# Routing tokens of two mixture-of-experts layers by scatter into expert regions of DRAM, with resident expert weights

## The chip, the cores and the metric

The kernel runs on one core of a Trainium2 chip. The metric is the device time of one execution in microseconds. The core has a matrix engine (PE, with its weight loads shown as PEld), a vector engine (DVE, `V` in the code), a scalar engine (ACT, `S`), a general engine (POOL, `G`), and an engine that only issues transfers (SP); each works through its own queue in order. Below, "us" are microseconds from the start of the profiled span.

## The reference

The input is x, 16 batches of 128 tokens with 128 features, and a condition and a context of 77 tokens per batch. All is float32. Four blocks are added to x one after the other:

```python
x = x + xcond0(layernorm(x), cond, ctx)    # self-attention, cross-attention, gated FFN (GLU)
x = x + ffn0(layernorm(x))                 # 1 shared + 7 routed experts, 2 of the 7 per token
x = x + xcond1(cond, ctx, layernorm(x))    # slot attention over the context, 3 turns
x = x + ffn1(layernorm(x))                 # 8 experts, 1 per token
```

An expert of ffn0 is `silu(h @ g.T) * (h @ u.T) @ d.T` with 352 inner features, weighted per token by the two scores normalised to one. An expert of ffn1 is `relu(h @ W1 + b1) @ W2 + b2` with 512 inner features, weighted by the largest softmax probability. Only the chosen experts have to be computed for a token.

## The kernel before, in words

The residual x is held on chip as `r`, 128 partitions by 16 batches by 128 features, and is worked on in four groups of four batches. After both attentions (to about 433 us) come, for each group, the GLU (`glu`, L1283) and the routing of ffn0 (`moe0_route`, L930); the routing of group g-1 is written after the GLU of group g. Then come the sort of all tokens by expert (`sort`, L757), the shared expert on the four groups (`moe0_shared`, L958), the tiles of the routed experts (`tiles`, L879), the slot attention (`slot_turns`), the routing of ffn1 (`moe1_route`, L1194), its sort and its tiles. Outside of what a program line demands, the framework that builds the program orders instructions on each engine; it also puts in the waits.

Routing a group (`normed`, L733) normalises it into a staged tile `st`, transposes it, multiplies by the router's weights and forms one-hot rows of the chosen experts (`oh`); `any` is their sum and `cum` a running count. `rows` (L746) writes the staged rows to a DRAM table (`tok0`, `tok1`) in token order, by SP; each row ends with the token's weight, and in ffn1 also holds the residual.

`sort` needs all four groups. Two matmul calls give every token its rank among those of its expert. Each expert's list is padded to full tiles of 128, which makes at most 38 tiles in ffn0 (2 x 2048 tokens over 7 experts) and 23 in ffn1 (2048 over 8). From rank and expert start comes the place of each token. The inverse list, which token stands at each place, is formed by one-hot rows over the lanes (`la`, L827) and products (`tv`, L817 and L822) as bf16 matmuls. Its results are `to`, the row that a tile's output goes to, `frm`, the row its input comes from, and `row`, the row of its expert's weights. In ffn1 two strings of matmuls into a scratch tile (`busy`, L798), whose results are not used, stand between its steps.

A tile j then has this path. `fetch` (L867): POOL gathers its 128 rows by an indirect transfer (L874); in ffn0 12 are issued ahead of the loop, in ffn1 6. `weights` (L855): SP loads the expert's row number into a register (L861) and issues a 576 KB load of that expert's weights (L864) into one of six buffers. `turn` (L885): PE transposes the tile, ACT copies it out. `up`: in ffn0 (L972) 6 matmuls, a tanh on ACT and two DVE operations (`silu_gate`, L950); in ffn1 (L1224) 4 matmuls, two ReLU halves on ACT and two on DVE. `finish` (L890): the down product (3 or 4 matmuls), its scaling, the next `weights`, a POOL scatter of the results (L895) and the next `fetch`. In ffn0 the scaling is on ACT with `wk`, a column that DVE makes for each tile (L987); in ffn1 it is two DVE operations (L1248, L1249). The loop writes up of tile j, turn of tile j+1, then finish of tile j-1. In ffn0 results go to a table `res0` of two rows per token; `combine` (L915) reads both (`yg`) and adds them to `r` by matmuls with the identity, at the start of the slot attention. In ffn1 they go to the output.

In the tables, `gum` and `h1n` are the up products, `ynm` and `ynn` the down products, with m for ffn0 and n for ffn1; `zsm`, `zsn` are fetched tiles, `ysm`, `ysn` results.

Of the kernel before, what the change touches and what calls it, by code (L numbers as in the profile page):

```python
# [31 lines left out]
WBUFS = 6  # L32
WT = 1156
NTOK = B * P
FETCH = 7
# [22 lines left out]
def pixart_kernel(  # L58
# [61 lines left out]
    for b in range(2, B, 2):  # L120
# [13 lines left out]
    tok0 = dram.tile([NTOK, D + 1], F32, name="tok0")  # L134
    tok1 = dram.tile([NTOK, 2 * D + 1], F32, name="tok1")

    res0 = dram.tile([2 * NTOK + NT0 * P, D], F32, name="res0")

    y_row = const.tile([P, 2 * B + NT0], F32, name="y_row")
    G.iota(  # L140
        y_row, pattern=[[P, y_row.shape[1]]], base=0, channel_multiplier=1, allow_small_or_imprecise_dtypes=True
    )
    zero_sb = attc.tile([P, D], F32, name="zero_sb")
    G.memset(zero_sb, 0.0)
    dma(out=res0[0:P, :], in_=zero_sb)

# [489 lines left out]
    def wide(nm):  # L636
# [3 lines left out]
    wt = ctx.enter_context(tc.tile_pool(name="wt", bufs=WBUFS))  # L640
    rt = ctx.enter_context(tc.tile_pool(name="rt", bufs=1))
    slp = ctx.enter_context(tc.tile_pool(name="slp", bufs=1))
    ctxn = slp.tile([NC, B, D], F32, name="ctxn")
    dma(out=ctxn, in_=ctx_tok.rearrange("b n d -> n b d"))
    cb = slp.tile([P, B, D], F32, name="cb")
    dma(
        out=cb,
        in_=rows[0, R_COND * D : (R_COND + B) * D].partition_broadcast(P).rearrange("p (b d) -> p b d", d=D),
    )


    def glu_body(g, hT):
        u = ph.tile([P, 4, 512], F32, name=f"u{g}", tag="act")
        for c in range(4):
            ps = {}
            for j in (1, 0):
                ps[j] = wide(f"glu{g}_{c}_{j}")
                PE.matmul(ps[j], lhsT=gluw[:, 4 * j + c, :], rhs=hT, start=True, stop=True)
            ge = ph.tile([P, 512], F32, name=f"ge{g}_{c}", tag="gate")
            S.activation(ge, ps[1], AF.Gelu, bias=col(C_FFB1 + 4 + c))  # L660
            V.scalar_tensor_tensor(u[:, c, :], ps[0], col(C_FFB1 + c), ge, ALU.add, ALU.mult)
        y = psX.tile([P, 4, D], F32, name=f"yg{g}", tag="x")
        token_major(y, lambda c: u[:, c, :], lambda c: gluw[:, 8 + c, :], 4)
# [36 lines left out]

    jt = rt.tile([P, NTM], F32, name="jt")
    G.iota(jt, pattern=[[1, NTM]], base=0, channel_multiplier=0, allow_small_or_imprecise_dtypes=True)

    w_issue = []

    batch_row = rt.tile([P, 2 * B], F32, name="batch_row")
    G.iota(batch_row, pattern=[[-1, 2 * B]], base=2 * B, channel_multiplier=0, allow_small_or_imprecise_dtypes=True)
    lanes = rt.tile([P, P], BF16, name="lanes")
    G.iota(lanes, pattern=[[1, P]], base=0, channel_multiplier=0, allow_small_or_imprecise_dtypes=True)

    class Routed:


        def __init__(self, nm, ne, nk, w, w0, tok):
            self.nm, self.ne, self.nk, self.w, self.w0, self.tok = nm, ne, nk, w, w0, tok
            self.ws, self.zs, self.st = [], {}, {}
            self.b0, self.nb = 0, B
            nb = self.nb
            self.nt = n_tiles(nk * nb * P, ne)
            self.oh = self.tile([P, nk, nb, ne], "oh")  # L720
            self.any = self.tile([P, nb + 1, ne], "any")
            self.cum = self.tile([P, nb + 1, ne], "cum")
            V.memset(self.any[:, nb, :], 0.0)
            V.memset(self.cum[:, 0, :], 0.0)
# [7 lines left out]

        def normed(self, i, nm):  # L733

            g = self.b0 // 4 + i
            rg = r[:, 4 * g : 4 * g + 4, :]
            rs, mean = ln_stats(rg, P, 4, nm, g)
            self.st[i] = rt.tile([P, 4, D + 1], F32, name=f"st{nm}", tag="zst", bufs=2)
            z = self.st[i][:, :, :D]
            scale_shift(z, rg, rs, mean, 4)  # L740
            t = transpose_n(z, P, 4, nm, g)
            zT = rt.tile([P, 512], F32, name=f"zT{nm}", tag="zT", bufs=4)
            S.copy(zT, t.rearrange("p a b -> p (a b)"))
            return zT

        def rows(self, i):  # L746

            t = self.tok[4 * i * P : (4 * i + 4) * P, :].rearrange("(b p) d -> p b d", p=P)
            dma(out=t[:, :, : D + 1], in_=self.st[i])
            if self.nk == 1:  # L750
                dma(out=t[:, :, D + 1 :], in_=r[:, 4 * i : 4 * i + 4, :])
# [5 lines left out]
        def sort(self):  # L757

            nm, ne, nk, nt, nb = self.nm, self.ne, self.nk, self.nt, self.nb
            pr = psM.tile([P, nb + 1, ne], F32, name=f"rank{nm}", tag=t_tag(self.b0 // 4))  # L760
            PE.matmul(pr, lhsT=before, rhs=self.any, start=True, stop=False)
            PE.matmul(pr, lhsT=ones, rhs=self.cum, start=False, stop=True)

            ci = rt.tile([P, ne], I32, name=f"ci{nm}", tag="ci")
            V.tensor_scalar(ci, pr[:, nb, :], float(P - 1), None, ALU.add)
            V.tensor_scalar(ci, ci, 7, 7, ALU.logical_shift_right, ALU.logical_shift_left)
            sc = [rt.tile([P, 16], F32, name=f"sc{nm}{k}", tag=f"sc{k}") for k in range(4)]
            for t in sc:
                V.memset(t[:, :8], 0.0)
            V.tensor_copy(sc[0][:, 8 : 8 + ne], ci)  # L770
            for k in range(3):
# [3 lines left out]
            ends, starts = sc[3][:, 8 : 8 + ne], sc[3][:, 7 : 7 + ne]  # L775

            past = rt.tile([P, NTM, 8], F32, name=f"past{nm}", tag="past")[:1, :nt, :ne]
# [613 lines left out]
```

## Time and profile before

| | us |
|---|---|
| median of 10 runs | 886.54 |
| lowest and highest | 884.17, 891.89 |
| profiled execution, its time | 890.23 |
| profiled execution, its span | 888.2 |
| PE busy in the span | 818.1 (92%) |
| DVE busy | 592.1 (67%) |
| ACT busy | 442.7 (50%) |
| POOL busy | 346.5 (39%) |

The span by stages, from the timeline: attention to about 433, GLU and routing of ffn0 433 to 503, sort and shared expert to 539, tiles of ffn0 539 to 624.5, slot attention to 806, routing and sort of ffn1 to 827, tiles of ffn1 to 884.5, last scatter to 888.2.

A view of stretches gives, for each, the busy time and instruction count of each engine, the granted PE clock as a share of full speed, the mean busy share of the 16 DMA engines, and GB/s. A group is a line's instructions on one engine with one operation and form: what it writes and reads (out<-in), partitions by elements, the count, busy time and mean ns of one, and then the engine's idle time ahead of them with what ended it. The chain of waits goes back from the last instruction through what released each. "issue" is time of an instruction's own start that no wait explains. Names ending in q, like SPq, are an engine's queue: register and transfer-issuing instructions.

### The profile page before, as it was taken

To read this page: it belongs to the slowest core of one execution; us is meant where nothing else is said; L and a number is where in the kernel's file an instruction comes from. 1 tells how busy PE (TensorE), PEld (TensorE's weight loads), DVE (VectorE), ACT (ScalarE), POOL (GpSimd) and SP (SyncE) were. 2 spreads that over 40 slices of the span, in tenths; PEclk is the share of its full clock that TensorE was granted. 3 is DMA by queue.
4 is the path that set the end of the run, shared out by engine and by line. 5 is a ranking of instruction groups with operands and counts; after the bars stand their busy time and mean duration, and the time that the engine had idled before them with its cause. 6 is when DMAs were issued, how large, how long until landed. Compare 5 with 4: busy or idle time off the path is not lost.

```text
span 888.2 us, 16297 instructions
## 1 busy us (share of the span) xinstructions
PE 818.1 (92%) x5847; PEld 647.0 (73%) x5847; DVE 592.1 (67%) x1845; ACT 442.7 (50%) x950; POOL 346.5 (39%) x408
## 2 busy tenths in 40 slices
PE   6999999999999999999999979999958889996997
PEld 5688887877777777787666649999546666665886
DVE  4587766767856666777877865655376777877454
ACT  3666765656644545543422203444356776762232
POOL 2233423334412222332532046776252433431676
PEclk9899999999999999999999978999968998985799
DMA  8200000000000000000200145996300000002794
GB/s 314 81 2 1 1 2 1 1 1 1 1 1 1 1 1 1 1 1 1 77 3 23 61 148 157 334 330 229 104 0 1 1 1 1 13 24 85 286 349 141
DMA packets 29563, 61.82 MB, mean 70 GB/s; under 512 B 4266, under 2 KB 18045, under 8 KB 28843
## 3 DMA queue, kind: packets, MB, share of 16 engines
q1 hardware_dynamic: 25211, 51.70, 16.9%
q0 software_dynamic: 4272, 9.09, 3.3%
q8 instruction: 46, 0.75, 0.4%
q14 instruction: 34, 0.28, 0.1%
HBM read 54.01 MB, written 7.23 MB: 69 GB/s over the span
## 4 chain that ended last, share of the span: by engine, by line
PE 62%; DVE 20%; POOL 5%; DMA 5%; ACT 4%; issue 3%; SPq 0%; POOLq 0%; ACTq 0%; DVEq 0%
PE po L441 6%; PE pv L339 6%; PE te L431 5%; PE ya L451 5%; PE gum L978 5%; PE s L380 4%; PE pk L332 4%; PE pq L322 3%; PE s L389 3%; PE ynm L989 2%; DVE ri L412 2%; PE h1n L1231 2%; DVE e L405 2%; DMA res<-ysm,tom 2%; PE yg L485 1%
## 5 line engine op out<-in xcount | busy, mean ns | idle before, releaser
L416 POOL TENSOR_TENSOR e<-e,ri 128x1024 f32<-128x1024 f32 (+1 forms) x64 | 100.6, 1573 | 251.0 <-DVE ri L413 207.5
L400 DVE TENSOR_REDUCE mx<-s 128x8 f32<-128x1024 f32 (+1 forms) x64 | 64.4, 1007 | 48.4 <-PE s L389 39.6
L412 DVE TENSOR_REDUCE ri<-e 128x8 f32<-128x1024 f32 (+1 forms) x64 | 64.2, 1003 | 27.4 <-ACT e L408 26.4
L432 ACT COPY eT<-te 128x512 f32<-128x512 f32 (+1 forms) x96 | 56.3, 587 | 51.0 <-PE te L431 50.4
L431 PEld LDWEIGHTS te<-ident,e 128*128 128x128 f32 (+1 forms) x512 | 61.5, 144 | 19.6 <-issue 11.7
L431 PE MATMUL te<-ident,e 128*128 128x128 f32 (+1 forms) x512 | 74.8, 274 | 0.0
L322 PE MATMUL pq<-ha,wa 128*128 128x256 f32 x256 | 66.1, 394 | 3.8 <-DVE r L455 2.8
L441 PE MATMUL po<-eT,v 128*64 128x128 f32 (+1 forms) x1024 | 69.4, 277 | 0.0
L408 ACT ACTIVATE e<-e 128x1024 f32<-128x1024 f32 (+1 forms) x64 | 57.1, 892 | 24.5 <-DVE e L405 22.8
L441 PEld LDWEIGHTS po<-eT,v 128*64 128x64 f32 (+1 forms) x1024 | 58.0, 137 | 11.8 <-DVE eT L432 6.3
L405 DVE TENSOR_TENSOR e<-s,mx 128x1024 f32<-128x1024 f32 (+1 forms) x64 | 63.8, 997 | 2.0
L451 PEld LDWEIGHTS ya<-wa,oT 128*128 128x128 f32 x512 | 60.8, 192 | 3.9 <-issue 1.4
L451 PE MATMUL ya<-wa,oT 128*128 128x128 f32 x512 | 62.6, 275 | 0.0
L978 PE MATMUL gum<-zTnm,wm 128*128 128x128 f32 x456 | 61.3, 275 | 0.1
L978 PEld LDWEIGHTS gum<-zTnm,wm 128*128 128x128 f32 x456 | 56.8, 192 | 0.4 <-ACT zTnm L888 0.2
L322 PEld LDWEIGHTS pq<-ha,wa 128*128 128x128 f32 x256 | 45.8, 196 | 12.1 <-DVE r L455 4.2
L874 POOL DMA_INDIRECT zsm<-tok,frmm x38 | 36.8, 967 | 35.0 <-DVE secm L852 21.6
L343 ACT COPY v<-pv 128x512 f32<-128x512 f32 (+1 forms) x64 | 37.3, 585 | 23.2 <-PE pv L339 23.2
L445 ACT COPY oT<-po 128x512 f32<-128x512 f32 x47 | 27.1, 576 | 42.8 <-PE po L441 42.8
L895 POOL DMA_INDIRECT res<-ysm,tom x38 | 37.3, 981 | 16.8 <-ACT ysm L993 7.2
L380 PE MATMUL s<-k,ha 128*128 128x308 f32 x128 | 42.6, 436 | 0.0
L332 PE MATMUL pk<-ctxT,wa 128*128 128x154 f32 x256 | 40.2, 302 | 2.1 <-DVE r L455 2.1
(388 smaller groups left out, 1864.3 us busy)
## 6 DMA issues: line engine op xcount, KB each, us to landing
wm<-in_moe_w_dram SPq DMA_DIRECT2D x38, 576.0 KB, 5.4
wn<-in_moe_w_dram SPq DMA_DIRECT2D x23, 578.0 KB, 5.8
wa<-in_attn_w_dram SPq DMA_DIRECT2D x4, 1024.0 KB, 8.5
ygm<-res SPq DMA_DIRECT2D x8, 256.0 KB, 3.3
tok<-stm SPq DMA_DIRECT2D x4, 258.0 KB, 3.0
tok<-stn SPq DMA_DIRECT2D x4, 258.0 KB, 3.0
x<-in_x_dram SPq DMA_DIRECT2D x8, 128.0 KB, 8.2
cb<-in_rows_dram SPq DMA_DIRECT2D x1, 1024.0 KB
```

What stands on the lines that cost most here:

```text
L322: PE.matmul(pq[:, j, :], lhsT=wqk[:, w : w + P], rhs=hT, start=True, stop=True)
L332: PE.matmul(pq[:, j, :], lhsT=wqk[:, w : w + D], rhs=kvT, start=True, stop=True)
L380: PE.matmul(ps[:, par, : 4 * nk].rearrange("p (j k) -> p j k", k=nk), lhsT=st["qT"][:, i * P : (i + 1) * P], rhs=st["kT"][:, h0 : h0 + 4, ...
L400: V.tensor_reduce(self.mx, self.ps, AX.X, ALU.max)
L405: V.tensor_tensor(self.e, self.ps, self.mx.unsqueeze(3).to_broadcast([P, 2, 4, nk]), ALU.subtract)
L408: S.activation(self.e, self.e, AF.Exp, scale=1.0 / math.sqrt(DH))
L412: V.tensor_reduce(self.ri, self.e, AX.X, ALU.add)
L416: G.tensor_tensor(self.e, self.e, self.ri.unsqueeze(3).to_broadcast([P, 2, 4, self.nk]), ALU.mult)
L431: PE.transpose(t[:nk, j, :], e[:, par, j, :], ident)
L441: PE.matmul(po[par * DH : (par + 1) * DH, j, :], lhsT=st["v"][:nk, i, 8 * hg + 2 * j + par, :], rhs=eT[:nk, par, j, :], start=True, stop=True,
L451: PE.matmul(y, lhsT=oT[:, c, :], rhs=st["wo"][:, 1024 + c * D : 1024 + (c + 1) * D], start=(c == 0), stop=(c == 7),)
L978: PE.matmul(ps[j][:, c * P : (c + 1) * P], lhsT=w[:, k : k + P], rhs=zT, start=True, stop=True)
```

## The change

The tokens are put in the order of their experts by the write to DRAM, in place of the gather.

Regions. `tok0` and `tok1` go. `disp0` (15360 rows of 520 B, 8 MB) and `disp1` (17408 rows of 1032 B, 18 MB) have a region of 2048 rows for each expert. One DMA on SP for each, behind the first loads, fills them at the start with zeros and a last column `NONE`, an index past every table's end. `res0` loses its spare rows.

Per group. `normed` writes a second copy of z (ACT, ffn0), and the staged tile's last column gets the token's output row (`staging`, DVE). `rank` finds the slots of the group's tokens from `cum` so far; `send` scatters the group's rows to their experts' regions: 8 POOL scatters in ffn0, 4 in ffn1.

After the groups. `plan` takes the place of `sort`: totals, tile ends, each tile's first row (`first`) and its weights' column (`row`). There is no inverse list, no `la` or `tv`, and no `busy`.

Weights. `load` brings all experts of a layer into one resident tile `wall` (7 x 590 KB after the attention; 8 x 592 KB written after ffn0's tiles, in the same buffer). For each tile, DVE copies the up part (768 columns in ffn0, 516 in ffn1) and ACT the down part (384, 640) out of it, at an address that each has loaded into a register.

Tiles. `fetch` is an SP register load and a plain 128-row DMA, 6 ahead. The loop's order is fixed on each engine: turn of tile j+2, up of j, finish of j-2. The scatter's index comes with the row; `wk` goes. The second half of up and the transposes have PSUM tiles of their own.

Small changes: the row addition to `cb` (4.52 us on POOL at L1053) is a `row_add` on four groups of 32 partitions; the context is in four tiles; work tiles move between pools; ffn1's weights are laid out as W1, b1, W2, b2.

```diff
-WBUFS = 6
-WT = 1156
+WBUFS = 3
+UP0, DN0 = 768, 384
+UP1, DN1 = 516, 640
-FETCH = 7
+FETCH = 6
+ZBUFS = 8
+NONE = 1 << 20
...
+    def dispatch(nm, ne, nt, pairs, w):
+        rows_ = -(-(ne * NTOK + (nt * P - pairs)) // (P * 4)) * P * 4
+        t = dram.tile([rows_, w], F32, name=f"disp{nm}")
+        pad = attc.tile([P, 4, w], F32, name=f"pad{nm}")
+        V.memset(pad, 0.0)
+        V.memset(pad[:, :, w - 1 :].bitcast(I32), NONE)
...
+            S.copy(st[:, 1, :, :D], z)
             return zT
...
+        def rank(self, i):
+            pr = psM.tile([P, 4, ne], F32, name=f"rank{nm}", tag=t_tag(i))
+            PE.matmul(pr, lhsT=before, rhs=self.any[:, gs, :], start=True, stop=False)
+            PE.matmul(pr, lhsT=ones, rhs=self.cum[:, gs, :], start=False, stop=True)
+            V.tensor_tensor(at, pr, ebase[:, :ne].unsqueeze(1).to_broadcast([P, 4, ne]), ALU.add)
+            V.tensor_tensor(oh, oh, at.unsqueeze(1).to_broadcast([P, nk, 4, ne]), ALU.mult)
+            V.tensor_reduce(sl, oh, AX.X, ALU.add)
+            V.tensor_copy(self.to, sl)
+
+        def send(self, i):
+            for b in range(4):
+                for k in range(self.nk):
+                    G.indirect_dma_start(
+                        out=self.sent[(4 * i + b) * self.nk + k],
+                        out_offset=bass.IndirectOffsetOnAxis(ap=self.to[:, k, b : b + 1], axis=0),
+                        in_=self.st[i][:, k, b, :], in_offset=None,
+                    )
...
+            for part in range(2):
+                self.address(part)
+                for _ in range(WBUFS):
+                    self.weights(part)
+            for _ in range(FETCH):
+                self.fetch()
...
+                self.at[part] = (V, S)[part].value_load(
+                    self.row[0:1, j : j + 1], min_val=0, max_val=(self.ne - 1) * self.wn
+                )
...
+            (V.tensor_copy, S.copy)[part](w, self.wall[:, bass.ds(self.at[part] + part * self.up, n)])
+            self.ws[part].append(w)
+            self.address(part)
...
+            row = nc.sync.value_load(self.first[0:1, j : j + 1], min_val=0, max_val=self.disp.shape[0] - P)
+            dma(out=z, in_=self.disp[bass.ds(row, P), :])
...
+            with tc.manual_schedule():
+                ys4 = psX.tile([P, 4, D], F32, name=f"yn{self.nm}", tag="x")
+                for j in range(2):
+                    turn(j)
+                for j in range(nt + 2):
+                    if j + 2 < nt:
+                        turn(j + 2)
+                    if j < nt:
+                        acts[j] = up(self.ws[0][j], zT[j], f"{self.nm}{j}", j)
+                        self.weights(0)
+                    if j >= 2:
+                        finish(j - 2)
...
+    m0.load()
...
     m0.tiles(moe0_up, moe0_down)
+    m1.load()
     slot_prologue()
```

## The prediction

> **What bounds the kernel now.** I read the stretches first (the columns are stretch and length, then busy time and instructions of PE, PEld, DVE, ACT, POOL, then PE clock, DMA share, GB/s), because the two routed layers are the only part that the change rebuilds.
>
> ```profile
> 425.00:483.00 58.00, 56.28 (x326) 38.36 (x327) 43.53 (x172) 18.81 (x29) 24.54 (x40) 1.00 0.12 39
> 503.00:521.00 18.00, 13.88 (x69) 8.43 (x68) 17.76 (x77) 2.21 (x5) 0.00 (x0) 0.81 0.21 67
> 521.00:539.00 18.00, 15.19 (x68) 12.06 (x66) 7.24 (x22) 1.19 (x2) 13.50 (x14) 0.72 0.55 179
> 539.00:586.00 47.00, 46.94 (x418) 46.64 (x419) 28.60 (x67) 22.33 (x66) 33.83 (x35) 1.00 0.86 287
> 586.00:606.00 20.00, 18.42 (x161) 17.85 (x160) 11.20 (x25) 8.01 (x25) 15.13 (x17) 1.00 0.94 314
> 806.00:827.00 21.00, 13.36 (x61) 11.11 (x60) 14.24 (x101) 4.12 (x11) 5.10 (x9) 0.50 0.42 126
> 827.00:884.50 57.50, 52.66 (x392) 47.76 (x391) 28.93 (x93) 20.53 (x69) 42.36 (x43) 0.96 0.81 286
> ```
>
> The GLU (425 to 483) and the first tiles (539 to 586) are PE's. From 503 to 521 DVE is the full one: that is the first sort. From 806 to 827 nobody is full and the PE clock is 0.50: the second sort, a string of small steps. In the last stretch PE idles 5 us and POOL does 42. Next, the chain of waits at the first sort (start, length, what):
>
> ```profile
> 518.69 0.59 DVE gss L955
> 520.90 0.21 issue
> 521.11 1.23 POOL zsm L874
> 525.14 6.71 DMA zsm<-tok,frmm
> 533.53 4.65 PE ym L485 x20
> 542.95 0.67 PE ynm L989 x6
> ```
>
> The shared expert's gate (L955) runs only when the sort lets DVE go; then a gather's landing (6.71) holds DVE once more, since wk (L987) waits for it in DVE's queue ahead of the shared work. So the shared expert, ready since 483, ends at 538.2, and the tiles start at 539.6. Last, the groups (busy and mean ns of one, then idle time before it by releaser):
>
> ```profile
> L895 POOL DMA_INDIRECT res<-ysm,tom x38 | 37.3, 981 | 16.8 <-ACT ysm L993 7.2 <-issue 4.0 <-ACT zTnm L888 1.8
> L874 POOL DMA_INDIRECT zsn<-tok,frmn x23 | 22.4, 975 | 19.0 <-DMA wn<-in_moe_w_dram 12.3 <-issue 4.6 <-PE ynn L1246 0.9
> L955 DVE SCALAR_TENSOR_TENSOR gsm<-thm,gum 128x384 f32<-128x384 f32 x38 | 21.1, 554 | 25.1 <-ACT thm L953 25.1
> L987 DVE TENSOR_SCALAR wk<-zsm,sgnm,secm 128x1 f32<-128x1 f32 x38 | 10.2, 269 | 8.6 <-ACT ysm L993 4.5 <-DMA zsm<-tok,frmm 4.1
> L227 DVE TENSOR_SCALAR stm<-r,ym,mvm 128x128 f32<-128x128 f32 x16 | 5.3, 343 | 2.4 <-POOL mvm L198 2.4
> L888 ACT COPY zTnm<-gum 128x128 f32<-128x128 f32 x37 | 9.8, 264 | 13.8 <-PE gum L886 13.4 <-PE gum L978 0.4
> L432 ACT COPY eT<-te 128x512 f32<-128x512 f32 x64 | 37.7, 590 | 0.0
> L1092 DVE TENSOR_TENSOR i<-i,eqs 128x512 f32<-128x512 f32 x4 | 2.7, 683 | 3.0 <-ACT i L1091 3.0
> L861 SPq TENSOR_LOAD <-row_latem x36: 263/270/390, 522.3 to 610.0; - x36
> ```
>
> A POOL indirect transfer takes 0.98 us and, by the timeline's starts (522.65, 523.89, 525.14), one is issued each 1.25 to 1.28. Two a tile are 2.55. PE needs less: six matmul passes take 0.67, so a pass is 0.112; a tile of the first layer has 12 + 6 + 1 = 19 passes, 2.12 us, and one of the second 8 + 8 + 1 = 17, 1.90. The first layer outruns POOL only while its 12 early gathers last.
>
> **The change, part by part.** Times go by the profiled execution: 890.2 us, of which 888.2 span. It lies 3.7 above the median of 886.5; I sum differences and take them off the median.
>
> *Start of the first tiles.* The sort's 20 us of DVE go (503 to 521 almost whole), as does wk. In come per group a rank (two matmul calls, four DVE ops of 0.2 to 0.3 us), a second copy of z on ACT (0.59 by L432), and on POOL 8 scatters, 8 x 1.28 = 10.2. POOL's own statistics between 449 and 482 are some 3 us a group and a group comes each 12.3 us, so POOL is just full: statistics wait up to 3 us behind sends, covered by PE's shared gates, and sends end late. Group 2's start after 490 and end near 501 to 508; group 3's slots are known near 504, so they end near 504 + 10.2 = 514 to 518.5. The landing of a scatter is 2.6 (the last, from its end at 885.6 to the span's, 888.2), and the tile's first load about 3.3 (the yg loads after the tiles): z at 520 to 524.5. PE's need from 483 is four groups of 12 x 0.43 + 24 x 0.107 = 7.7, and routers of 3, so 517 at the least. DVE does 22 fewer us of sort, 4 for the plan and some 3 for the first copies. I take 527 where it was 539.6: **-12**, between -3 and -20.
>
> *The first layer's loop.* POOL falls to one scatter, 1.28 a tile. SP keeps 0.27 + 0.17 (two small register steps on the same line, 152 and 18 ns) + 0.34 (the issue at L864) = 0.8 per load. The new load on the others, which no row shows, is a copy of weights from the resident tile with an address in a register. For DVE, 768 columns: L987 to L227 gives 0.58 ns a column, hence 0.72; by L227 to L1092, 0.91. With two gates of 0.554: 1.82 to 2.02 a tile, under 2.12. ACT's 384 columns (L888 to L432, 0.85 ns each) are 0.48; with 0.264, 0.498 (L953) and 0.367 (L993), 1.61. The register load itself is 0.27 + 0.17 = 0.44 by SP's rows; I take it at nothing, hidden under the copy queued before it, as the engine's queue reads ahead. Without that cover DVE needs 2.26 to 2.46 and becomes the bound. With it: 38 x 2.12 + 1.5 = 82 against 84.4: **-2.5**, between +7 and -3. Steps two apart give each DVE or ACT wait a whole tile of PE work.
>
> *Between the layers.* The second layer's resident weights (8 x 592 KB = 4.7 MB) wait for the last copy out of the first's and go ahead of the yg loads on SP. At the 330 GB/s of the busiest slices that is 14 us, begun some 6 us before the tiles end, so yg lands near 9 us after, where its first use was 8 to 10 after: **+1**, 0 to +5.
>
> *Start of the second tiles.* The one-hot's last group is ready at 813.5, the first at 803. Scatters are 16 x 1.28 = 20.5 us plus 3.3 of statistics on POOL: from 805 they end at 829 at the latest, and 816 + 5.1 = 821 at the earliest. With 2.6, 3.3 and 0.8 for transpose and copy, the first up is at 828 to 836; before it was 827.9. I take **+5**, 0 to +8, near the later end because every group comes after 803. PE's clock stays low there in both.
>
> *The second layer's loop.* PE 1.90. DVE: 2 x 0.346 (L1238) + 0.291 (L1248) + 0.353 (L1249), with 516 columns at 0.57 to 0.69: 1.91 to 2.03, a little more than PE. So 23 x 1.97 + 2 for the slow clock at first + 1.5 for the tail = 49 against 56.4: **-7.5**, between +2 (register load uncovered, 2.40 a tile) and -9.5.
>
> *Pads.* 26 MB go out during the attention, where DMA moves 1 to 3 GB/s; they stand behind all first loads on SP. 0 taken; 26 MB at 314 GB/s are 83 us, none of it waited for before 460, and the attention's operands are on chip: 0 to +2. The memsets (under 2.5 us) lie under the wait for x. The 4.5 us cb op and the dummy matmuls go: 0, POOL waited for nothing there, and the clock was 0.50 in spite of them.
>
> Sum: -12 - 2.5 + 1 + 5 - 7.5 = -16, so **870** from the median.
>
> **Two rules weighed.** DVE's copies beside POOL's transfers: four DVE ops (L227, 77x128) that ran beside the first gathers took 1.23 us in sum and 1.10 after, and the gathers kept their 0.94 and their step. The Trainium skill's page "SBUF — State Buffer", section "Who interferes with whom", speaks against the change: fp32 copies in DVE's two-port mode shut GpSimd out, its descriptors included. By that rule each copy would push the scatter back by its own length, which POOL at 1.28 of 2.12 could still bear. The register load is 270 ns on SP here; "DMA: Bandwidth & Descriptors", section "Latency and other measured facts", gives about 600 ns as its floor. By that figure an uncovered load would cost 0.33 a tile more than above.
>
> **Rivals.**
> 1. *Register load and copy stand in series on DVE* (slower). For it: DVE has 0.1 to 0.3 us to spare beside PE, and no row shows a load overlapped with work of its own engine. Against: SP's loads ran while its queue moved on. Price at SP's rows: +7 in the first loop instead of -2.5, +2 instead of -7.5, so +3: 889.5. At twice that load, 2.8 a tile: 61 x 2.8 + 5 for edges = 176 against 140.8 of both loops now, less 6 elsewhere: +29, 916. It decides from 61p + 5 = 146.8, a mean step of 2.32 us.
> 2. *POOL's sends take the sort's place.* If the sends also hold up the statistics of later groups, the first tiles start at 536 and the second at 836: -3 - 2.5 + 1 + 8 - 7.5 = -4, 882. For it: POOL is full by my count from 465 to 518. Against: PE has shared gates to do meanwhile.
> 3. *Larger gain.* First tiles at PE's own bound, near 519 (-20), second start unchanged, both loops at PE's pace (-12), +1 between: -31, 855.5. For it: sends could go out earlier than I place them.
> 4. *The change doesn't do what it says*: the fixed order makes PE wait on a transpose whose load is late, or the shared work stands behind the first copies; steps of 2.4 to 2.55 through the waits, by the sum of rival 1 +5 to +14: 891 to 900.
>
> **How the numbers follow.** Chances: forecast 0.45 (863 to 877), larger gain 0.15, sends 0.10 (0.02 of it within the bound), series on DVE 0.25 (0.05 within the bound), order 0.05. About 0.3%, 2.7 us, is what a measurement can tell from no change. Faster 0.45 + 0.15 + 0.08 = 0.68; same 0.02 + 0.05 = 0.07; slower 0.20 + 0.05 = 0.25. The range 852 to 896 takes in the larger gain's middle and the series at SP's rows; above it lies about half of the series' slow side, 0.12, below it 0.05.
>
> **What would show it.** Right: no DVE stretch full from 503 to 521; first up near 527 and near 833; steps of 2.1 and below 2.05; POOL below 70% in both loops; DVE's weight copy at 0.7 to 0.9 us with idle gaps by PE around it. Wrong: DVE without gaps in the loops, a step above 2.3, gaps named after the queue; POOL full until the first tiles and PE idle before them; a yg load in the chain; long records for the statistics of the attention while the pads go out.

## The result, and the profile after

The changed kernel takes 926.24 us (median of 18 runs, 917.67 to 929.27); the kernel before took 886.26 beside it (62 runs). The ratio is 1.0433, with a 95% interval from 1.0414 to 1.0451: slower by 40 us, where the forecast was 870. The profiled execution took 927.35, of which 925.6 is span; the span before was 888.2. The difference of 37.4 us, by marks on PE that mean the same in both kernels:

| stage (us) | before | after | forecast | measured |
|---|---|---|---|---|
| start of the span to the GLU | 434.4 | 435.6 | 0 to +2 | +1.2 |
| GLU to the first up product of ffn0 | 105.2 | 108.3 | -12 | +3.1 |
| to the last down product (first loop) | 84.1 | 86.2 | -2.5 | +2.1 |
| to the first slots | 24.4 | 35.2 | +1 | +10.8 |
| to the last one-hot group of ffn1 | 165.2 | 170.0 | +5, with the next | +4.8 |
| to the first up product of ffn1 | 14.6 | 19.3 | | +4.7 |
| to the last down product (second loop) | 55.7 | 59.2 | -7.5 | +3.5 |
| to the end of the span | 4.6 | 11.8 | not named | +7.2 |

No stage gained. Differences in one part of the fifth stage are not put down to any edit: from the first slots to the first one-hot group, where the change rebuilds nothing, the kernel before took 154.7 us at a granted PE clock of 0.87, the changed one 150.1 at 0.88, and four of its variants about 142 at 0.94. From the first one-hot group to the first up product of ffn1, which is the second start, it is 25.1 before and 39.2 after, +14.1. First the stretches of the changed kernel (stretch and length, then busy time and instructions of PE, PEld, DVE, ACT, POOL, then PE clock, DMA share, GB/s):

```profile
425.00:483.00 58.00, 51.65 (x300) 34.57 (x296) 38.44 (x146) 16.95 (x26) 24.73 (x38) 0.98 0.26 92
483.00:503.00 20.00, 15.07 (x68) 9.77 (x68) 11.95 (x61) 3.78 (x7) 10.72 (x15) 0.84 0.08 28
503.00:521.00 18.00, 15.88 (x83) 11.22 (x84) 13.31 (x66) 3.78 (x8) 7.42 (x10) 0.86 0.06 19
521.00:539.00 18.00, 11.29 (x29) 5.60 (x28) 9.52 (x29) 3.92 (x7) 11.55 (x14) 0.81 0.16 47
560.00:606.00 46.00, 45.23 (x404) 44.85 (x403) 33.52 (x65) 29.59 (x86) 24.93 (x21) 1.00 0.23 60
835.00:855.00 20.00, 3.98 (x15) 3.32 (x16) 6.25 (x39) 5.88 (x14) 8.36 (x8) 0.50 0.27 86
855.00:914.00 59.00, 50.29 (x388) 46.73 (x386) 35.20 (x111) 30.66 (x87) 21.47 (x22) 0.96 0.22 60
```

What the change removes is gone: DVE is no longer full from 503 to 521 (13.3 of 18), DMA falls below a quarter in the loops, POOL to 54% of the first and 36% of the second. But before the tiles PE stands still: 6.4 us up to 483, 4.9, 2.1 and 6.7 in the next three stretches (1.7, 0.5, 4.1 and 2.8 before the change), and its granted clock falls to 0.84 from 483 to 503, where it was 1.00:

```profile
483.00:503.00 20.00, 19.53 (x91) 11.66 (x90) 16.75 (x75) 5.65 (x11) 3.32 (x8) 1.00 0.09 27
```

And from 835 to 855 nobody works: PE 4.0 of 20. What ended PE's waits, and DVE's, from 430 to 545 in the changed kernel (engine and line, what it waited for: total, times, longest), and last the first two of DVE's waits in the kernel before:

```profile
PE tm L259 <- DVE stm L243: 6.9, 1, 6.9
PE gu L967 <- DVE gss L957: 6.7, 2, 4.3
PE glu L682 <- DVE u L685: 5.2, 1, 5.2
```

```profile
DVE stm L243 <- POOL mvm L214: 9.5, 4, 7.1
DVE zc L243 <- POOL mvc L214: 7.6, 2, 6.1
DVE stn L754 <- DMA dispm<-stm,tom: 5.9, 2, 5.0
```

```profile
DVE stm L227 <- POOL mvm L198: 2.4, 4, 1.0
DVE zc L227 <- POOL mvc L198: 2.9, 2, 1.4
```

PE's 18.8 us come from DVE, and DVE's 23 mostly from sends: `mvm` (routing, L214) and `mvc` (the slot attention's context, hoisted into this stretch) are made on POOL, where 2.4 and 2.9 have become 9.5 and 7.6, and `stn` (L754) is the copy of row numbers into a staging tile of the *second* layer, hoisted as well, which waits until sends from that buffer have landed. POOL's timeline shows what stands ahead of the statistics (start, length, what, idle before):

```profile
499.13 0.96 POOL L797 DMA_INDIRECT dispm<-stm,tom  x1 [0.30 <-issue]
500.39 0.96 POOL L797 DMA_INDIRECT dispm<-stm,tom  x1 [0.30 <-issue]
501.37 0.22 POOL L205 TENSOR_TENSOR mvm<-stm 128x4 f32<-128x4 f32 x1
...
504.49 0.20 POOL L214 TENSOR_TENSOR mvm<-mvm,ym 128x4 f32<-128x4 f32 x1
513.42 1.09 POOL L797 DMA_INDIRECT dispm<-stm,tom  x1 [8.73 <-DVE stc L200]
```

These are the end of group 1's eight sends (491.4 to 501.4) and the first of group 2's. Group 3's statistics waited for the rest of the train, its normalisation for them, the router for that; and since DVE works in order, the shared expert's gates (L957) waited too. Trains run from 469.95 to 480, 491.4 to 501.4, 513.4 to 523.4 and 525.6 to 535.7, and the chain of waits follows them. POOL itself is not full: it stands idle for 6.42 us before the second train and 8.73 before the third, waiting for DVE as DVE had waited for it.

Some groups of the first loop (540 to 640; busy and mean ns of one, idle before):

```profile
L897 POOL DMA_INDIRECT res<-ysm,zsm x38 | 44.4, 1167 | 51.7 <-ACT ysm L989 50.3 <-ACT wqc L1061 1.0 <-ACT wkq L1062 0.4
L957 DVE SCALAR_TENSOR_TENSOR gsm<-thm,gum 128x384 f32<-128x384 f32 x38 | 21.1, 554 | 18.0 <-ACT thm L955 17.5 <-ACT zTnm L890 0.4
L866 DVE COPY w0m<-wallm 128x768 f32 x35 | 19.4, 553 | 0.0
L866 ACT COPY w1m<-wallm 128x384 f32 x35 | 17.6, 502 | 0.0
```

The gates take what they took; the new copies are 0.553 and 0.502, behind other work of their engines (no idle before them), and DVE waits between for PE's products by way of ACT: this loop is PE's.

SP between the layers, then PE's waits from 800 to 856, and the second of them in the kernel before:

```profile
626.18 5.30 SPq L847 DMA_DIRECT2D walln<-in_moe_w_dram  x8
636.67 16.41 SPq L927 DMA_DIRECT2D ygm<-res  x8
```

```profile
PE tnn L888 <- DMA zsn<-dispn: 15.1, 2, 14.8
PE rankn L782 <- DVE anyn L1203: 12.5, 1, 12.5
```

```profile
PE rankn L761 <- DVE anyn L1210: 4.0, 1, 4.0
```

The second layer's weights do go ahead of the yg loads, and their first use comes at 649.1 (633.7 before). At the second start PE waits 12.5 us for the last group's one-hot (DVE waited 5.2 for POOL's statistics behind the first two groups' sends, and 3.3 for a landing), and then 14.8 for the first load (the last eight sends, landing, load).

The second loop, DVE and then ACT over one step of 2.60 us:

```profile
877.18 0.29 DVE L1239 TENSOR_TENSOR ysn<-ynn,w1n 128x128 f32<-128x128 f32 x1 [0.34 <-PE h1n L1225]
877.51 0.35 DVE L1240 SCALAR_TENSOR_TENSOR ysn<-ysn,zsn 128x128 f32<-128x128 f32 x1
877.78 0.60 DVE L1232 TENSOR_SCALAR an<-h1n,w0n 128x128 f32<-128x128 f32 x2
879.02 0.43 DVE L866 COPY w0n<-walln 128x516 f32 x1 [0.63 <-ACT an L1230]
879.78 0.29 DVE L1239 TENSOR_TENSOR ysn<-ynn,w1n 128x128 f32<-128x128 f32 x1 [0.33 <-PE h1n L1225]
```

```profile
877.57 0.73 ACT L866 COPY w1n<-walln 128x640 f32 x1 [1.18 <-DVE ysn L1239]
878.20 0.26 ACT L890 COPY zTnn<-tnn 128x128 f32<-128x128 f32 x1
878.35 0.63 ACT L1230 ACTIVATE an<-h1n,w0n 128x128 f32<-128x128 f32 x2
```

Nobody is full; it is a ring. DVE's `ysn` frees a down buffer (it reads the bias in it), ACT copies into it, then transposes out and does its ReLUs; these free an up buffer, DVE copies into that, loads the next register (0.33 of idle, put down to PE), and only then comes to the next `ysn`, which stands behind the copy in the written order.

### The profile page after: what moved, and what is told of

Same layout as the page of the kernel before. It is cut to its first block, busy times and chain, and to the rows that moved or that the text cites. A ratio compares the mean times of both kernels' runs of the same rounds, so it can differ in the third digit from the quotient of the medians.

```text
span 925.6 us, 16690 instructions
## 1 busy us (share of the span) xinstructions
PE 809.8 (87%) x5799; PEld 640.5 (69%) x5799; DVE 602.2 (65%) x1827; ACT 472.6 (51%) x1017; POOL 338.6 (37%) x392
## 4 chain that ended last, share of the span: by engine, by line
PE 52%; POOL 15%; DVE 14%; issue 12%; ACT 3%; DMA 3%; POOLq 1%; SPq 0%; DVEq 0%; ACTq 0%
PE po L457 6%; PE pv L355 6%; PE te L447 5%; PE ya L467 5%; PE s L396 4%; PE pq L338 4%; PE pk L348 3%; POOL res L897 3%; POOL dispm L797 3%; PE s L405 3%; POOL out_dram L897 2%; DVE ri L428 2%; DVE e L421 1%; PE su L1138 1%; PE ys L1166 1%
## 5 line engine op out<-in xcount | busy, mean ns | idle before, releaser
L448 ACT COPY eT<-te 128x512 f32<-128x512 f32 (+1 forms) x96 | 56.4, 587 | 51.0 <-PE te L447 50.4
L457 PEld LDWEIGHTS po<-eT,v 128*64 128x64 f32 (+1 forms) x1024 | 58.0, 137 | 11.8 <-DVE eT L448 6.3
L897 POOL DMA_INDIRECT res<-ysm,zsm x38 | 44.4, 1167 | 51.7 <-ACT ysm L989 50.3
L979 PE MATMUL gum<-zTnm,w0m 128*128 128x128 f32 x456 | 57.2, 275 | 0.0
L979 PEld LDWEIGHTS gum<-zTnm,w0m 128*128 128x128 f32 x456 | 54.2, 192 | 0.0
L359 ACT COPY v<-pv 128x512 f32<-128x512 f32 (+1 forms) x64 | 37.4, 586 | 22.9 <-PE pv L355 22.9
L797 POOL DMA_INDIRECT dispm<-stm,tom x32 | 31.6, 986 | 26.9 <-DVE stc L200 11.4
```

The lines of the kernel that those rows point to most:

```text
L457: PE.matmul(po[par * DH : (par + 1) * DH, j, :], lhsT=st["v"][:nk, i, 8 * hg + 2 * j + par, :], rhs=eT[:nk, par, j, :], start=True, stop=True,
L897: G.indirect_dma_start(out=wrote[j], out_offset=bass.IndirectOffsetOnAxis(ap=zs[j][:, self.width - 1 :].bitcast(I32), axis=0), in_=ys, in_ ...
L979: PE.matmul(ps[j][:, c * P : (c + 1) * P], lhsT=w[:, k : k + P], rhs=zT, start=True, stop=True)
```

## Experiments

Marks are given as in the table. Each run is one execution, the last one ten; a number in brackets is its span. The stages are compared with the changed kernel's, and diffs are cut to the lines that matter.

**Load after yg.**

```diff
-    m1.load()
     slot_prologue()
     slot_turns(range(4), m0.combine)
+    with tc.issue_after(m0.last_yg):
+        m1.load()
```

> The only change to the changed kernel: the 4.7 MB of the second layer's weights stand behind the eight yg loads on SP's queue, not ahead of them. Theory (the yg loads wait in line): the stretch from the last down product of the first layer to the first tq product of the slots falls from 35.2 us to the 24.5 of the kernel before, 1 or 2 more for weights that now load beside it; span 925.6 to 914-917. Rival (the landing of the last scatters, or the combining itself, sets this stretch): it stays above 33 and the span above 923.

Measured 926.46 (span 924.0). Last down product to first slots: 29.8 where it was 35.2. The queue is half of the 10.8. The rest, by the traces, is the slot prologue's ten weight products (`product`, one chain of PE, ACT and DVE): in the changed kernel they run at the loop's end and after it, from 627 to 636; the kernel before had seven of them beside the sort and the shared expert (507 to 540) and three between its last tiles (622 to 625). Runs below move them.

**Copy last in the step.**

```diff
                     acts[j] = up(self.ws[0][j], zT[j], ...)
-                    self.weights(0)
                 if j >= 2:
                     finish(j - 2)
+                self.weights(0)
```

> The only change to the changed kernel: in the tile loop the copy of the next up weights stands behind finish of tile j-2 on DVE, not between up and finish. Theory (a ring through two queues sets the second layer's step: DVE's bias sum lets ACT's weight copy go, behind that stand ACT's transposed copy and ReLUs, these let DVE's weight copy go, behind that stands the next bias sum): the step falls from 2.60 to 2.0-2.15 us, the span by 9 to 13, to 913-917; the first layer's step stays at 2.12. Rival (register load and copy in series on DVE are the price, whatever the order): the step stays at 2.5 or more, the span above 923.

Measured 917.86 (916.2). Second loop 50.5 where it was 59.2 (55.7 before the change), the first hardly changed at 86.7 (86.2). The median step of the second loop falls from 2.59 to 1.90, PE's own pace by the prediction. The ring is open: DVE's next `ysn` no longer stands behind the copy.

**Fixed expert.** Every tile uses the first expert's weights, so the register loads are left out.

```diff
-   if j < self.nt:
+   if False:
        self.at[part] = (V, S)[part].value_load(...)
...
-   (V.tensor_copy, S.copy)[part](w, self.wall[:, bass.ds(self.at[part] + part * self.up, n)])
+   (V.tensor_copy, S.copy)[part](w, self.wall[:, part * self.up : part * self.up + n])
```

> The changed kernel with the weight copies from a fixed address, without the register loads on DVE and ACT: every tile uses the first expert's weights. Theory (a register load on DVE is not hidden under the copy ahead of it; it costs the 0.33 us that stand between the copy and the next DVE operation in the second layer's ring): step of the second layer 2.60 to 2.27, of the first unchanged at 2.12, since DVE has room there; span 917-919. Rival (the load is read ahead, the 0.33 is a wait for PE): the step stays at 2.55 or more, span above 923.

Measured 916.58 (913.9). Second loop 52.8, 0.28 a tile less; first loop 85.4 against 86.2, so there the load was under PE. It is exposed only where the copy is a link of the ring.

**No sends in the first layer.** The first layer's dispatch is left out (its results are zeros).

```diff
-                for k in range(self.nk):
+                for k in range(self.nk if self.nk == 1 else 0):
                     G.indirect_dma_start(out=self.sent[...], ...)
```

> The changed kernel without the 32 sends of the first layer: no token reaches an expert there, its tiles work on the pads and scatter nothing; everything else is issued (the result table is zeroed as a whole at the start). Queuing the sends one group later did not help: statistics then met a train of eight that was already running. Theory (the trains of 10 us on POOL hold statistics, and through DVE's order the shared expert): without them PE has no wait above 2 us between 440 and 540 and the first up product comes at 520-527 where it was 543.9, so 17 to 23 us of the stage are the sends' price. Rival (the rank and plan work on DVE and the hoisted index copies are the price): first up after 535.

Measured 899.27 (897.4). GLU to first up 88.4 where it was 108.3, the first up at 522.0: 32 sends cost 20 us of a stretch in which they were to lie beside PE. PE's waits of 18.8 are down to 0.3 for the gates and 0.6 for the normalised tile; the GLU's 5.2 is gone.

**Sends later.** Context statistics ahead of the first layer, and each group's sends behind the next group's statistics.

```diff
         zT = R.normed(i, nm)
+        if i:
+            R.send(i - 1)
...
-        R.send(i)
...
+    ctx_stats.extend(ln_stats(ctxn[g], NC, 4, f"c{g}", f"c{g}") for g in range(4))
```

> Changes to the changed kernel: the context's statistics are taken ahead of the GLU groups, and a group's eight sends of the first layer are queued on POOL behind the next group's statistics, not ahead of them (two result buffers fewer make the room). Theory (sends stand ahead of statistics on POOL, DVE waits in order for these, PE for DVE): the idle times of PE of 5.2 and 6.9 us before 505 go, DVE has no wait above 2 us on POOL between 460 and 510, the first up product of the first layer comes at 528-534 where it was 543.9; span 912-916. Rival (32 sends of 1.27 us are themselves too many, or DVE's wait on landed sends at 525 is the whole cause): first up after 540, span above 921.

Measured 923.63 (921.9), first up at 548.7, 5 us later, not earlier. Place in the program is not place in time: the sends moved by one group meet the group after (DVE waited 12.7 us for `mvm` in all), and the last train ends at 538.5. The mend failed: the wait stayed, and moved by a group.

**The second layer's sends behind later groups' statistics**, and its staging copies behind the ranks.

```diff
+        for k in ((), (0,), (), (1, 2))[i]:
+            R.send(k)
-        st = R.staging(i)[:, 0]
+        with tc.issue_after(R.ranked):
+            st = R.staging(i)[:, 0]
...
-        R.send(i)
+        if i == 3:
+            R.send(i)
```

> Changes to the changed kernel: the second layer's index copies into the staging tiles (DVE, L754) are held back behind each group's ranks, and its sends are queued on POOL behind the statistics of the next group, those of groups 1 and 2 behind those of group 3. Theory (DVE waits in order, 5.0 and 0.9 us in the first layer and 3.3 in the second, for landed sends because these copies stand early in its queue; and two statistics of 1 us stand behind eight sends): first up product of the first layer 3 to 5 us earlier; from the first any of the second layer to its first up 28-32 us where it was 39.1; span 911-916. Rival (the 16 sends in a row set this stretch): it stays above 36, and the first layer's start moves by less than 1; span above 921.

Measured 915.0 (913.3). From the first one-hot group to the first up: 34.9 where it was 39.2, above the expected 28 to 32 and below the rival's 36; the kernel before took 25.1. So about a third of the 14.1 is the order, and the rest stays: PE still waits 14.5 us for the first load. The whole stage from the first slots on is 179.8 where it was 189.3, but 5.1 of this lie ahead of the first one-hot group (145.0 for 150.1), and the two runs with early gathers, which leave the second layer alone, show 181 for the stage; so the edit is not worth 9.5. In the first layer the start moved by 1.8, less than the 3 to 5 expected.

**Bounds check on the kernel before.** To see whether the scatters' bounds check makes the closing drain long.

```diff
-   **({} if self.nk == 2 else dict(bounds_check=NTOK - 1, oob_is_err=False)),
+   bounds_check=(2 if self.nk == 2 else 1) * NTOK - 1, oob_is_err=False,
```

> The kernel before with one edit: the scatters of the first layer have a bounds check as well, so that padded rows are left out and not written to the spare rows. After the changed kernel's last scatter has landed, POOL's closing drain lasts 10.2 us where it was 3.07, in every profile. Theory (bounds-checked or left-out rows pile up work on POOL that the drain pays at the end: 61 checked scatters in the changed kernel, 23 before): the drain grows to about 10, the span by 6 to 8 to 894-897, and a scatter of the first layer keeps its 0.98 us. Rival (the drain belongs to something else in the changed kernel, the sends or the large index of the pads): it stays near 3, span 887-891.

Measured 929.62 (927.7), beside 930.72 for the kernel before in the same round. Its drain is 3.07 us, as without. The theory fell.

**Four mends together**: load after yg, copy last, and the routing's and context's statistics by Newton steps on DVE in place of POOL; the second layer's staging copies late.

> The changed kernel with four mends together: the yg loads ahead of the second layer's weights; the weight copy behind finish; the statistics of both routings and of the context wholly on DVE (the -0.5 power by an integer seed and three Newton steps, 11 small operations, where POOL had one); the index copies of the second layer held back behind the ranks (one result buffer fewer for the room). Theory (each wait falls by itself): first up of the first layer 526-532, the stretch to the first tq product 30, from the second layer's first any to its first up 30-33, its loop 50-52; span 880-890. Rival (the sends bound both starts by their sum on POOL): first up after 538 or that second stretch above 36, span above 897.

Measured 901.8 (900.1). The second loop (50.8) and the stretch between the layers (29.5) kept what the single edits had given, and the second start took 34.1 from the first one-hot (39.2 in the changed kernel, 30 to 33 expected). The first up did not follow: 542.1. With POOL's statistics gone, DVE still stood for 5.15 us up to 478.3, at the copy of row numbers into group 3's staging tile (L763 there, three buffers), hoisted and waiting for group 0's sends to land.

**Index copies late.** The same, with that copy behind its group's rank.

```diff
         R.rank(i)
+        with tc.issue_after(R.ranked):
+            R.index(i)
```

> The three edits of the run before (second resident load behind the yg loads, copy last in the step, statistics of routing and context on DVE) and one more: in the first layer the index copy into the staging tile is placed behind that group's rank, where the run before had it early in DVE's queue, waiting 5.15 us for group 0's sends to land. Theory (DVE's queue is held by waits on sends, first through POOL's statistics, then through this copy): group 3's places, 523.2, come 4 to 6 us earlier, the first up at 535 to 538.5 where it was 542.1, the whole 895 to 899 where it was 901.8. Rival (the wait was covered; PE and the slow clock near 515 set group 3's places): first up 540.5 to 543, the whole 900 to 903.

Measured 901.21 (899.5). First up at 534.7; GLU to first up 98.6, almost 10 less than the changed kernel's 108.3. The whole hardly moved: 3.4 us of the shared expert's last matmuls now stand in the loop (87.0), and the stretch to the first one-hot group, which the edit leaves alone, took 3.3 more. From the GLU to the last down product it is 185.6 against 192.0 in the run before, 194.5 in the changed kernel and 189.3 before the change.

**No sends in the second layer.** Its dispatch is left out (its tiles find padding rows, and write nothing).

> The changed kernel without the second layer's 16 sends (the second layer's dispatch is left out: its tiles find only padding rows, and their scatters write nothing). Theory (at the second start the sends stand ahead of POOL's statistics, and then the last of them and its landing stand ahead of the first tile): the one-hot's first to last group in 10 to 12 us as before the change (19.9 with sends), from the last to the first up 9 to 12 (19.3 with sends); first up at 836 to 840 where it is 854.6. Rival (the start is late because of the index copies or ACT, not the sends): first up 850 or later. Closing drain of POOL: if it takes 0.08 us for each transfer that POOL has issued (10.20 with 109, 7.585 with 77), 8.9; if it goes with the results' scatters, 10.2 or another number.

Measured 900.72 (899.0). First to last one-hot group 12.7 (19.9 with sends), from there to the first up 10.2 (19.3): 16 sends cost 16 us. The closing drain is 8.880, as the count foretold.

**Prologue ahead.** The run with late index copies, the slot prologue (products and contexts) written ahead of the first tiles.

> The run with the late index copies, and two more edits: the slot prologue's products and contexts are written ahead of the first tiles, where PE waits for the first load, in place of after them; and the first weight copies are written behind the shared expert. Theory (after the tiles the prologue's chain is late, and the shared expert's last matmuls stand behind the transposes): from the last down product to the first slots 20 to 24 us where it was 29.5; first up 1 to 4 earlier than in the run with late index copies; the whole 884 to 891. Rival (the prologue takes PE, ACT and DVE from the last sends and the first loads): first up 2 to 5 later, the whole 893 to 898.

Measured 902.72 (901.0). Last down product to slots 22.7, as expected; but the first up at 549.2, 14.5 later. The rival was right, and larger than I put it: the last send ended at 528.7, about as in the run before (529.1), but 11 us of context matmuls (537 to 548) stood ahead of the tiles in PE's fixed order.

**Extra gathers.** The run before it, with 13 gathers more in the first loop.

> The run before it with 13 gathers more on POOL, one beside every third tile of the first layer, into a tile that nobody reads: 122 transfers by POOL, as many as the kernel before had, in place of 109. Theory A (the closing drain clears what POOL's transfers have left in a store that is cleared on its own after some number between 109 and 122, since the kernel before with 122 drained in 3.07 us, the changed one with 109 in 10.20): 2 to 4 us. Theory B (0.08 us for each transfer): 11.2 to 11.4. Theory C (gathers clear themselves, scatters don't, or something else than a count): 10.2. First loop: POOL 1.28 us a tile and 2.55 each third, mean 1.7 under 2.1, so up to +2; the whole 6 to 7 less than the run without the gathers by A, 1 to 3 more by B and C.

Measured 904.66 (903.0). The drain fell from 10.192 to 3.087, as theory A had it; the loop, 5.7 us longer with the gathers, and the stretches beside it took that back, so the whole did not fall by the expected 6 to 7.

**13 and 26 gathers early**, on the changed kernel itself, in the GLU's stretch.

> The changed kernel with 13 gathers more on POOL, early in the GLU, into a tile that nobody reads: 122 transfers in place of 109. A count that starts again somewhere between 109 and 122: closing drain 3.0 to 3.2 us. An effect of gathers among the first tiles' scatters: 10.2 to 11.3. The time falls by about 7 less what POOL's statistics lose to the gathers (0 to 8).

> The same with 26 gathers: 135 transfers. A count that starts again: 13 more than with 122, so 3.09 + 13 x 0.082 = 4.1 to 4.2. A store emptied for good once it has been full: 3.1. An effect of place: 10.2 or above.

Measured 924.80 (922.4) and 937.79 (936.1). The drains, of the changed kernel, of it without the second layer's sends, and with 13 and 26 gathers more (instructions; shortest/median/longest in ns):

```profile
L1378 POOLq DRAIN  x3: 45/113/10200, 914.6 to 925.4; - x3
```

```profile
L1378 POOLq DRAIN  x3: 45/113/8880, 889.3 to 898.7; - x3
```

```profile
L1385 POOLq DRAIN  x3: 45/113/3088, 918.5 to 922.1; - x3
```

```profile
L1385 POOLq DRAIN  x3: 45/113/3665, 931.6 to 935.8; - x3
```

Of the three theories a count that starts again comes nearest, but its step does not fit: 3.665 lies between the 4.1 to 4.2 of that theory and the 3.1 of a store emptied for good. 77, 93 and 109 transfers give 7.585, 8.880 and 10.200, 0.082 each; 122 give 3.07 to 3.09 in five kernels (the one before among them); 13 gathers more add 0.58, 0.044 each and not 0.082. Beside that, 13 gathers made group 0's first send leave at 482.0 instead of 469.95, and the first up come at 556.2 instead of 543.9: 12.1 later in, 12.3 later out. (All write one tile, so most wait until the one before has landed, and one leaves every 2.7 to 3.7 us.) With 26 the first up comes at 568.7. In this order POOL's queue is the path.

**All mends**: those of the run with late index copies, except that the second layer's statistics stay on POOL with its sends behind them; the first weight copies behind the shared expert, the prologue's products (not its contexts) ahead of the tiles, and 13 early gathers.

> All mends: load of the second resident weights behind the yg loads; copy last in the step; routing and context statistics of the first layer on DVE; index copies behind the ranks; second layer's sends behind the statistics of later groups; first weight copies behind the shared expert; the slot prologue's products ahead of the first tiles, its contexts after them; and 13 extra gathers on POOL before the first sends (122 transfers in all). If the terms add up: GLU to last down product 186 to 189 (185.6 with late index copies, plus 1 to 3 for the products), then 23 to 26 to the first slots (29.4), 178 to 182 from there to the second layer's first up (185.1), 50 to 52 for its loop, 4.7 to 5.2 at the end (11.8): span 879 to 888, time 881 to 890, against 886 of the kernel before. Rival (something unnamed keeps it slower): span above 892.

Measured 885.85 us (10 runs) beside 886.67 for the kernel before (13 runs): ratio 0.9992, interval 0.9962 to 1.0022. The terms add up (span 882.4): GLU to last down product 185.4 and 21.0 to the slots (both below what was expected), 184.2 to the second first up (above the 178 to 182), 50.4 for the loop, 5.1 at the end. PE's waits from 430 to 529 in this run:

```profile
PE tnm L905 <- DMA zsm<-dispm: 5.0, 3, 4.0
PE ym L510 <- DVE ma L977: 1.8, 1, 1.8
PE yg L510 <- DVE u L694: 0.9, 1, 0.9
```

Where DVE held PE for 18.8, it is 2.7: the first layer's routing no longer asks POOL for anything but sends. The early gathers delay the first send here too (480.6; 469.2 with late index copies), but POOL stands idle for 1.05 and 0.69 us before the last two trains, waiting for DVE, and the last send ends at 522.8 (529.1): they no longer set the end. No run takes them out of this kernel. Its second start is still 34.5 us from the first one-hot group, 9.4 more than before the change; 7.3 less from the GLU to the slots and 5.3 less in the second loop make up for it.

## Why the prediction was wrong

**Start of the first tiles (-12, measured +3.1): the step that failed.** The sentence is "statistics wait up to 3 us behind sends, covered by PE's shared gates". The start missed by 15.1 us, the largest of the misses (second loop 11.0, between the layers 9.8, the end 7.2). I had POOL full by my own count and then priced the meeting of its two kinds of work by means. A train of eight sends is 10.1 us in which POOL does nothing else, and a group's statistics come when they come: DVE waited 7.1 and 6.1 at once. Nor was there cover: the gates need DVE, and DVE was the one that waited. I also missed the third wait, staging copies that stand in DVE's queue until sends have landed. Group 3's places were known near 525, not 504 (the sums were ready at 519.7 and stood behind such a copy), and the last train ended at 535.7 where I had 514 to 518.5. The run without sends gives the forecast's price: its first up is at 522.0. Rival 2 named this mechanism, at 0.10, and was still too low: it priced sends that end late (536, 836), not that all behind DVE is late with them (543.9, 854.6).

**First loop (-2.5, measured +2.1).** The step is 2.12 as forecast and PE's: 84.4 busy of 86.2. The 86.2 hold 2.4 us of the shared expert's last matmuls, which had come late, so this is the first term's debt. The copies were cheaper than I took them (0.554 for 768 columns, not 0.72 to 0.91), and the register load was hidden, as the run with a fixed expert shows.

**Between the layers (+1, measured +10.8).** Half is the queue order that I named and put at the wrong size: the yg loads left at 636.7, 10.5 us after the weights' first, and their first use moved by 15.4 (649.1 for 633.7). The other half, a prologue that no longer runs ahead of the tiles and between them, I had not looked for; 5.3 us remain when the load is moved, and with the products ahead of the tiles the stretch is 21.0 to 23.9, under the 24.4 of the kernel before.

**Start of the second tiles (+5, measured +9.5).** Right in sign; the start itself, from the first one-hot group, is +14.1, and the 9.5 come out by luck, because the slots ahead of it ran 4.6 us shorter. The size missed the same wait as at the first start, statistics behind trains (12.5 us of PE). Without sends it is 16 us less.

**Second loop (-7.5, measured +3.5).** The "1.91 to 2.03, a little more than PE" was DVE's sum of busy times, and no engine's busy time sets this step: DVE is busy 35.2 of 59. The ring through both engines' copies does, 2.60; opened, the step is 1.90. Rival 1 put register load and copy in series on DVE and said that a mean step of 2.32 decides; the mean of both loops is 2.30, just under it. The first loop's 2.12 spoke against it, the second's 2.60 for it, but the copy's place in the ring was worth more (0.38 a tile) than the load (0.28, taken away alone; the two overlap).

**The end (not named, +7.2).** POOL's closing drain. It took 3.07 us before (884.4 to 887.5, so the 2.6 that I read as the last scatter's landing lie mostly under it), and I had not looked at what it depends on.

**Pads.** Measured +1.2 up to the GLU, inside 0 to +2. "POOL below 70%" and "no DVE stretch full" came true, and were no signs of a gain.

On the two rules: POOL's scatters beside DVE's 768-column copies took 1.167 us in the mean (0.981 before the change, 0.984 in the second loop). This agrees in direction with the Trainium skill's page "SBUF — State Buffer", section "Who interferes with whom", which lets such copies shut GpSimd out; with 0.30 to the next transfer POOL still had 0.65 of each 2.12 to spare, so I take it to have cost no time; no run isolates it. The page "DMA: Bandwidth & Descriptors", section "Latency and other measured facts", gives about 600 ns as the floor of a register load; here one takes 0.27 us on SP, and the exposed part on DVE is 0.28 to 0.33, so the measurement decides.

## What to carry to other kernels

An engine that issues indirect transfers is taken for the whole train: before moving work onto its queue, list what else that engine makes, who waits for it in which in-order queue, and price the meeting at the train's full length, not at a mean. Where a loop's copies refill buffers that other steps of the same loop read, draw the ring of "frees" and "waits" through both engines and add up one turn of it; busy sums can lie well below. Gains count only if what was late next is looked up too: here five separate terms had to be mended before the scheme was level with what it replaced.

## What the runs showed of the hardware

An indirect transfer of 128 rows holds POOL for 0.94 to 0.98 us and 0.30 more to the next one, whether it gathers or scatters; the first of a train took 1.09 to 1.23 in the changed kernel, and beside the 768-column copies it was 1.17 in the mean. POOL's last DRAIN grows by 0.082 us for each indirect transfer issued (7.585, 8.880, 10.200 us for 77, 93, 109) and is back at 3.07 to 3.09 with 122, at 3.665 with 135; 13 useless gathers shorten it by 7 us. Where the count starts again, and why the step after it is 0.044, was not settled.
